# Finishing the last image of a quantised convolution block: the channel gate from sums of numerators, the last product in halves

## The chip, the cores and the metric

The kernel runs on one core of one Trainium2 chip, as one launch. The metric is the device time of one execution in microseconds. The text names the engines as the profile does: PE is TensorE, ACT is ScalarE, DVE is VectorE, POOL is GpSimd, SP is SyncE, which issues most DMAs.

## The reference

The input is `x` of shape (16, 256, 28, 28). It is normalised in 32 groups of channels, and the layer is added to `x`. Twice, a 3x3 convolution is replaced by a soft look-up: for each channel the nine values of a patch are compared with 16 centroids, a softmax over the 16 gives weights, and the weighted centroids go through a matrix.

```python
def amm_conv3x3(x, centroids, w_sub, stride=1):
    ...
    d = sum(p * p) - 2.0 * einsum('bncs,cks->bnck', p, centroids) + sum(centroids * centroids)
    attn = softmax(-d, axis=-1)
    lut = einsum('cks,cso->cko', centroids, w_sub)
    out = einsum('bnck,cko->bno', attn, lut)

def se_layer(x, w1, b1, w2, b2):
    s = mean(x, axis=(2, 3))
    s = relu(s @ w1 + b1)
    s = sigmoid(s @ w2 + b2)
    return x * s[:, :, None, None]

# y is x normalised by groups
out = relu(bn1(amm_conv3x3(y, centroids1, wsub1)))
out = bn2(amm_conv3x3(out, centroids2, wsub2))
out = relu(se_layer(out, se_w1, se_b1, se_w2, se_b2) + y)
return x + out
```

What matters here is the end of an image in the second layer: the gate `s` needs the mean of every output channel over the whole image, so it can start only when the whole image is summed up, or when those sums are got in another way. They can be: the mean over positions of a product of weights and numerators is the product of the weights and the summed numerators.

## The kernel before, in words

The 16 images are done one after the other, first all of layer one, then all of layer two. An image is four blocks: two halves of the rows (14 rows, `N` = 392 positions) times two halves of the input channels. For each block TensorE makes the logits (`lg`), ScalarE the exponentials (`e`), TensorE the sums of the denominators (`nb`) and of the numerators (`na`), VectorE the reciprocals (`r`, spread by `rb`), and VectorE, ScalarE and GpSimd the scaled numerators: nine tiles of 128 x 392, held in pairs (`qp`) and one single (`qo`).

The numerators of the four blocks then go through the weight matrices. Instead of eight block products (two row halves, two input halves, two output halves) the kernel does seven and some sums and differences, in the manner of Strassen and Winograd: `PRODUCTS` lists them (A11, S1, S3, S2, S4, A12, A22), each 9 matmuls of 128 x 392 in f32, which the profile counts as 18. GpSimd makes the differences of numerators (`mix`). The results are added up in the four regions of an image: `c11` and `c12` are the two row halves of the first 128 channels, `c21` and `c22` those of the other 128. The last two products are A12, which completes `c11`, and A22, which completes `c21`.

The schedule is written out by hand: `at(cluster, sub, function, ...)` files a step under a place in time, and the steps are issued in the order of the places. Each engine works through its own queue in that order. `g` is the first cluster of an image (8 an image), so a step of image `b` at `g + 12` stands in the middle of the next image's work, or, for the last image, at the end of all. PSUM is a ring of four tiles of two banks each (`p_ring`, tags `ps0` to `ps3`); `banks` picks the tag from `ROLES` and the step, or from `tag`, and a new tile waits until the old one of its tag has been read.

At the end of an image of layer two, `norm_out` or `norm_both` applies the batch norm on ScalarE and sums up the positions at the same time, `se_hidden` and `se_gate` make the gate (two small products on TensorE, activations on ScalarE), `se_recip` finishes the sigmoid on VectorE, `finish_norm` makes the group-normalised input again, and gate, sum, relu and final sum follow. For all images but the last this is spread over the products of the next one: `finish_gate` and `finish_relu` on ScalarE, `finish_sum` and `finish_add` on GpSimd. For the last image nothing is left to hide it, and `finish_fast` does it on VectorE in two passes for each half of the channels.

`gn_var` makes the group norm's scale: a small product, two short steps on VectorE, then the power -1/2 and a product on GpSimd. `flags` checks on VectorE that sums and centroids lie in the range for which the fast path holds; `flag_sum` adds the flags up. Every engine loads the result and branches past a fallback, which redoes everything in a safer form and does not run here.

Of the kernel before, what the change touches and what calls it, by code (L numbers as in the profile page):

```python
# [17 lines left out]
P = 128  # L18
H = W = 28
HW = H * W  # L20
# [3 lines left out]
N = RT * W  # L24
PTW = RT * PW
K = 16
S = 9
NS = 9
NST = 18
GN_EPS = 1e-5  # L30
# [8 lines left out]
KO = (2, 3, 4, 5, 6, 7, 8, 0, 1)  # L39
# [45 lines left out]
def kernel(  # L85
# [20 lines left out]
    nc = tc.nc  # L106
    B, C, _ = x.shape
    NB = C // P
# [28 lines left out]
    def bank(name, step=None, role=None, tag=None):  # L137
        return banks(name, step, role, tag)[:, 0, :]
# [28 lines left out]

    xs = {}

    def load_x(b, spare=False):  # L170
        if spare:
            t = epool.tile([P, 4, N], F32, tag="e", name="e").rearrange("p i n -> p (i n)")
            t = t.rearrange("p (b n) -> p b n", b=NB)
# [101 lines left out]
    def rsqrt(dst, src, eps, n):  # L275
        t = small.tile([P, n], F32, name="rs_t")
        nc.gpsimd.tensor_scalar(t, src, eps, None, op0=ALU.add)
        nc.gpsimd.tensor_tensor(dst, t, mhalf[:, :n], ALU.pow)
# [4 lines left out]
    bn = []  # L283
# [12 lines left out]

    cst = const.tile([P, 64], F32, name="cst")

    def small_bank(name, step):
        return bank(name, step, step and ROLES["small"][step % 2], EARLY["small"].get(step))  # L300

    def center_sq(wf, c0, w, eng=None):
        sq = rpool.tile([P, N], F32, tag="r", name="sq")
# [56 lines left out]
    def gn_var(b, k0=0, n=NB, step=None):  # L360
        gm, dv = gst.pop((b, "m"))
        ps = small_bank("gnp", step)[:, :n]
        nc.tensor.matmul(ps, lhsT=gmat, rhs=dv[:, :n], start=True, stop=True)  # L363
        var = small.tile([P, NB], F32, name="gn_var")
        neg = small.tile([P, NB], F32, name="gn_neg")
        nc.vector.tensor_scalar_mul(neg[:, :n], gm[:, :n, 0], -1.0)
        nc.vector.scalar_tensor_tensor(var[:, :n], ps, GN_EPS, gm[:, :n, 1], op0=ALU.add, op1=ALU.add)
        rstd, shift = (nrm[:, b, i, k0 : k0 + n] for i in (1, 2))
        nc.gpsimd.tensor_tensor(rstd, var[:, :n], mhalf[:, :n], ALU.pow)
        nc.gpsimd.tensor_tensor(shift, neg[:, :n], rstd, ALU.mult)  # L370

    def grid(t):
        return t.rearrange("p (r w) -> p r w", w=PW)
# [149 lines left out]
    def pair(u, mm):  # L523
        return qs["pair"][u["qi", mm]]
# [15 lines left out]

    accs = {}

    def product(key, us, w, ks, first=True, last=True, step=None):
        if first:
            accs[key] = bank("acc", step, step and ROLES["acc"][step % 2], EARLY["acc"].get(step))
        for n, k in enumerate(ks):
            nc.tensor.matmul(  # L547
                accs[key][:, :N], lhsT=wl[w][:, k, :], rhs=us["q", k],
                start=first and n == 0, stop=last and n == len(ks) - 1,
            )  # L550

# [278 lines left out]

    se = {}

    def se_hidden(b, step=None):
        ysum = ys[b, "sum"]
        ps = small_bank("sep", step)[: 2 * RED, :1]
        terms = [(k, i) for k in range(NB) for i in range(2 if b >= B - 1 else 1)]
        for k, i in terms:
            nc.tensor.matmul(  # L838
                ps, lhsT=w1_sb[:, k, :], rhs=ysum[:, k, i : i + 1],
                start=(k, i) == terms[0], stop=(k, i) == terms[-1],  # L840
            )
# [3 lines left out]
        nc.scalar.activation(se[b], halves, AF.Copy, scale=hid)  # L845

    def se_gate(b, step=None):
        ps = small_bank("sep", step)[:, :NB]
        nc.tensor.matmul(ps, lhsT=w2_sb, rhs=se[b], start=True, stop=True)  # L849
        gt = small.tile([P, NB], F32, name="se_gt")  # L850
        for k in range(NB):
            nc.scalar.activation(
                gt[:, k : k + 1], ps[:, k : k + 1], AF.Exp, bias=nb2_sb[:, k : k + 1], scale=-1.0
            )
        nc.scalar.activation(gt, gt, AF.Identity, bias=one, scale=1.0)
        se[b] = gt
# [8 lines left out]
    def finish_norm(b, k):  # L865
        if k == 0:
            if b == B - 1:
                ys[b, "t"] = epool.tile([P, 4, N], F32, tag="e", name="xn").rearrange("p i n -> p (i n)")
            else:
                ys[b, "t"] = io.tile([P, 1568], F32, tag="pb", name="xn")  # L870
        nc.scalar.activation(
            ys[b, "t"][:, HW * k : HW * k + HW], xs[b][:, k], AF.Identity,
            bias=nrm[:, b, 2, k : k + 1], scale=nrm[:, b, 1, k : k + 1],
        )
# [12 lines left out]
    def finish_fast(b, k):  # L887
# [4 lines left out]
            ys.pop((b, "t"))  # L892
        nc.vector.scalar_tensor_tensor(y, y, 0.0, xs[b][:, k], op0=ALU.max, op1=ALU.add)

    def store(b, k, dst=None, eng=None):
# [20 lines left out]
        nc.vector.memset(fl[:, 3:4], 1.0)  # L916

    def flag_sum():
        ps = bank("flp")[:, :1]
# [5 lines left out]
    def at(cl, sub, f, *a, **kw):  # L925
        jobs.setdefault((cl, sub), []).append((f, a, kw))
# [24 lines left out]
    for j, u in enumerate(blocks):  # L951
# [41 lines left out]
        for mm in (4, *kept):  # L993
            at(g, 1.2, spread, u, mm)
            at(*((g, 1.3) if j != 1 else (5, 0.06)), scale_q, u, mm)

    for l in range(2):
        for b in range(B):
            n = l * B + b
# [2 lines left out]
            for c, w, r, ks in PRODUCTS:  # L1002
                if g + c == 5:
                    for sub, k0, k1 in ((0.8, 0, 5), (0.82, 5, 7), (0.84, 7, 9)):
                        at(4, sub, product, (n, c), us[r], w, ks[k0:k1], k0 == 0, k1 == 9, step=4)
                else:
                    at(g + c, 1.32 if g + c == 7 else 2.0, product, (n, c), us[r], w, ks, step=g + c)
            for mm in (1, 2, 3, 4, 0):
                at(g + 5, 2.5 if n else {4: 0.07, 0: 0.09}.get(mm, 0.05), mix, us[0], mm, us[1], us[0])
                at(g + 7, 1.35 if mm in (4, 0) else 1.25, mix, us[1], mm, us[2], us[1])  # L1010
                at(g + 8, 1.37 if mm == 1 else 1.4, mix, us[0], mm, us[2], us[0])
                at(g + 10, 1.4, mix, us[0], mm, us[0], us[3])
# [10 lines left out]
            at(g + 12, 0.0, acc_add, l, b, c11, (n, 11))  # L1023
            at(g + 12, 2.02, acc_add, l, b, c21, (n, 12), op=ALU.subtract)
            if l == 0 or b == B - 1:
                at(g + 11, 1.9, norm_out, l, b, *c12)
                at(g + 11, 1.91, norm_out, l, b, *c22)
                at(g + 12, 1.9 if l else 0.05, norm_out, l, b, *c11)
                at(g + 13, 1.06, norm_out, l, b, *c21)
            else:  # L1030
                for o in range(NB):
                    at(g + 12 + o, 1.9, norm_both, b, o)
# [17 lines left out]
                        at(*((g + 4, 1.92) if b else (4 + 3 * q, 1.6 + 0.05 * q)), to_home1, b + 1, q)  # L1050
            else:
                last = b == B - 1
                at(*((g + 11, 0.6) if last else (g + 13, 2.6)), load_x, b, last)
                at(g + 14 - last, 2.1, se_hidden, b, g + 14 - last)
                at(*((g + 14, 1.05, se_gate, b, g + 14) if last else (g + 17, 2.1, se_gate, b, g + 17)))
                at(*((g + 14, 1.05) if last else (g + 18, 0.3)), se_recip, b)
                for q in range(NB):
                    at(*((g + 12, 0.4) if last else (g + 19, 1.9)), finish_norm, b, q)
                    if not last:
# [5 lines left out]
                    else:  # L1065
                        at(g + 14, 1.92, finish_fast, b, q)
                        at(g + 14, 1.92, store, b, q)
                if b == B - 1:
                    at(g + 11, 1.9, flags)
                    at(g + 12, 2.9, flag_sum)  # L1070

    at(0, 1.55, load_w, 0, "A11")
# [247 lines left out]
```

## Time and profile before

| | us |
|---|---|
| median of 3 runs | 2622.66 (2621.62 to 2627.43) |
| profiled execution | 2625.73 |
| its span | 2624.2 |
| mean granted TensorE clock | 0.998 of full speed |

The profile gives each engine's busy time, the chain of work that ended last, groups of instructions with their mean duration and the idle time before them (with what ended it), and a timeline by engine. A group's row reads: line, engine, operation, out <- in, shapes, xcount, then busy us and mean ns of one, then the idle time before it and its releasers. A row of the timeline reads: start, duration, engine, line, operation, and in brackets the idle time just before. `L547` is line 547 of the kernel before. A row with q behind the engine's name is the work of its sequencer. Rows of stretches give the length, then the busy time of PE, PEld, DVE, ACT and POOL with counts, then the granted clock, the DMA share and GB/s.

### The profile page before, as it was taken

What the parts mean: (1) busy time and instruction counts of PE and PEld (TensorE: products, weight loads), DVE (VectorE), ACT (ScalarE), POOL (GpSimd) and SP (SyncE); (2) the same over time, 40 slices, a digit from 0 to 9 for tenths busy, and PEclk for the clock granted to TensorE, in tenths of its full rate; (3) what the DMA queues carried; (4) which work ended last, traced back from release to release, by engine and by line L of the source; (5) the groups of instructions that cost most, each with busy time, mean ns of one, the idle gap of its engine ahead of it and who ended that gap; (6) DMA issues with size and microseconds to landing.
All of it is one profiled execution on the core that took longest, in us unless ns stands there. A gap on an engine that the chain in (4) does not pass through costs nothing.

```text
span 2624.2 us, 85651 instructions
## 1 busy us (share of the span) xinstructions
PE 2588.2 (99%) x36984; PEld 1264.5 (48%) x36984; DVE 1762.8 (67%) x3774; ACT 1360.3 (52%) x1879; POOL 1893.1 (72%) x1286
## 2 busy tenths in 40 slices
PE   6999999999999999999999999999999999999997
PEld 2444454444544444544444444444444444444444
DVE  5776656666566665566676767766776667767665
ACT  5444544444444454444455655555655556555553
POOL 3786666766568766676666887878878777878786
PEclk9999999999999999999999999999999999999999
DMA  8656656666555565554664344444344443444441
GB/s 218 159 164 177 197 149 184 171 174 173 149 144 147 170 183 177 171 156 139 179 170 105 104 116 126 118 120 119 104 120 129 123 118 106 117 122 122 116 120 47
DMA packets 217960, 374.38 MB, mean 143 GB/s; under 512 B 29752, under 2 KB 188520, under 8 KB 217576
## 3 DMA queue, kind: packets, MB, share of 16 engines
q1 hardware_dynamic: 211256, 335.24, 47.8%
q0 software_dynamic: 6320, 33.58, 3.5%
q8 instruction: 295, 4.83, 0.8%
q14 instruction: 89, 0.73, 0.1%
HBM read 288.93 MB, written 79.80 MB: 141 GB/s over the span
## 4 chain that ended last, share of the span: by engine, by line
PE 97%; DVE 1%; ACT 0%; DMA 0%; POOL 0%; issue 0%; SPq 0%; DVEq 0%; POOLq 0%; ACTq 0%
PE acc L547 52%; PE lg L412 17%; PE nb L477 14%; PE na L463 14%; DMA pt<-home 0%; DVE r L505 0%; PE sep L849 0%; ACT e L423 0%; DVE gn_st L340 0%; POOL qp L556 0%; PE sep L838 0%; DMA xt<-in_x 0%; PE gnp L346 0%; PE gnp L363 0%; DVE rb L520 0%
## 5 line engine op out<-in xcount | busy, mean ns | idle before, releaser
L547 PE MATMUL acc<-qp,wall 128*128 128x392 f32 x3072 | 1096.9, 500 | 1.0 <-DVE qp L539 0.7
L423 ACT ACTIVATE e<-lg 128x784 f32<-128x784 f32 x960 | 737.8, 821 | 637.2 <-PE lg L412 634.3
L556 POOL TENSOR_TENSOR qp<-qp,qp 128x784 f32<-128x784 f32 x512 | 943.4, 1866 | 156.1 <-DVE qp L539 155.7
L547 PEld LDWEIGHTS acc<-qp,wall 128*128 128x128 f32 x3072 | 565.2, 190 | 508.6 <-issue 60.0
L520 DVE STREAM_SHUFFLE rb<-r 128x392 f32<-128x392 f32 x1024 | 551.2, 605 | 0.0
L412 PE MATMUL lg<-pt,wd 32*32 32x392 f32 x16256 | 484.2, 502 | 6.8 <-DMA pt<-home 4.4
L491 DVE SCALAR_TENSOR_TENSOR r<-nb,kst,r 128x392 f32<-128x392 f32 x128 | 80.0, 625 | 461.1 <-ACT r L487 445.7
L477 PE MATMUL nb<-e,cwb 64*32 64x392 f32 x8192 | 376.6, 492 | 0.1
L463 PE MATMUL na<-e,cwa 64*32 64x392 f32 x8192 | 374.3, 492 | 0.0
L539 DVE TENSOR_TENSOR qp<-na,rb 128x784 f32<-128x784 f32 x352 | 333.8, 972 | 60.0 <-PE na L463 48.5
L528 POOL TENSOR_TENSOR qo<-qo,rb 128x392 f32<-128x392 f32 x128 | 132.3, 1033 | 326.8 <-DVE rb L516 326.3
L505 DVE RECIPROCAL r<-r 128x392 f32<-128x392 f32 x128 | 333.2, 2603 | 4.4
L528 POOL TENSOR_TENSOR qp<-qp,rb 128x784 f32<-128x784 f32 x160 | 295.7, 1858 | 3.6 <-issue 0.7
L477 PEld LDWEIGHTS nb<-e,cwb 64*32 64x32 f32 x8192 | 189.9, 106 | 179.0 <-issue 26.3
L463 PEld LDWEIGHTS na<-e,cwa 64*32 64x32 f32 x8192 | 182.7, 106 | 182.5 <-issue 74.5
L412 PEld LDWEIGHTS lg<-pt,wd 32*32 32x32 f32 x16256 | 121.0, 103 | 282.6 <-issue 251.0
L547 PE MATMUL acc<-qp,w_A 128*128 128x392 f32 x512 | 182.6, 499 | 0.0
L487 ACT ACTIVATE r<-nb,kst 128x392 f32<-128x392 f32 x128 | 86.7, 677 | 164.6 <-PE nb L477 164.6
L447 POOL TENSOR_TENSOR z<-z,mx 128x1568 f32<-128x1568 f32 x32 | 91.8, 2869 | 94.7 <-DVE mx L441 94.7
L547 PE MATMUL acc<-qo,wall 128*128 128x392 f32 x384 | 157.7, 492 | 0.0
L533 ACT COPY qp<-na 128x784 f32<-128x784 f32 x160 | 130.0, 813 | 26.9 <-PE na L463 25.1
L547 PEld LDWEIGHTS acc<-qp,w_A 128*128 128x128 f32 x512 | 94.5, 190 | 82.3 <-DVE qp L539 19.8
(154 smaller groups left out, 1640.1 us busy)
## 6 DMA issues: line engine op xcount, KB each, us to landing
pt<-home SPq DMA_DIRECT2D x762, 209.0 KB
pt<-home SPq DMA_DIRECT2D x762, 104.5 KB
home<-xpad SPq DMA_DIRECT2D x30, 899.0 KB
xt<-in_x SPq DMA_DIRECT2D x30, 784.0 KB
out_dram<-y SPq DMA_DIRECT2D x32, 392.0 KB
d_wS<-st SPq DMA_DIRECT2D x12, 192.0 KB
wall<-d_wS SPq DMA_DIRECT2D x4, 576.0 KB
wall<-in_ws SPq DMA_DIRECT2D x3, 576.0 KB
```

Source lines behind the costliest of these rows:

```text
L412: nc.tensor.matmul(bk[32 * c : 32 * c + 32, :N].rearrange("p (r w) -> p r w", w=W), lhsT=wts["wd", u["hh"]][32 * i : 32 * i + 32, mm, c, : ...
L423: nc.scalar.activation(eg[:, 2 * i : 2 * i + 2, :], bk[:, :, :N], AF.Exp, scale=2.0)
L447: nc.gpsimd.tensor_tensor(zk, zk, mx.unsqueeze(2).to_broadcast([P, N // 4, K]), ALU.subtract)
L463: nc.tensor.matmul(bs[32 * i : 32 * i + 32, r, :N], lhsT=wts["cwa", u["hh"]][64 * r : 64 * r + 64, mm, i, :], rhs=es[64 * r : 64 * r + 64, ...
L477: nc.tensor.matmul(bs[32 * i : 32 * i + 32, r, :N], lhsT=wts["cwb", u["hh"]][64 * r : 64 * r + 64, mm, i, :], rhs=es[64 * r : 64 * r + 64, ...
L505: nc.vector.reciprocal(u["r"], u["r"])
L520: nc.vector.stream_shuffle(rb[:, r, :], u["r"], mask_of(2 * mm + r))
L528: nc.gpsimd.tensor_tensor(q, q, u.pop(("rb", mm)), ALU.mult)
L533: nc.scalar.copy(pair(u, mm), u.pop(("na", mm))[:, :, :N])
L539: nc.vector.tensor_mul(pair(u, mm), u.pop(("na", mm))[:, :, :N], rb)
L547: nc.tensor.matmul(accs[key][:, :N], lhsT=wl[w][:, k, :], rhs=us["q", k], start=first and n == 0, stop=last and n == len(ks) - 1,)
L556: nc.gpsimd.tensor_tensor(pair(out_u, mm), pair(in0, mm), pair(in1, mm), ALU.subtract)
```

## The change

It touches the last two images of layer two, and one short step of layer one.

- **Gate of the last image.** The sums of `c11` and `c21` over their positions are no longer taken from the finished regions. `norm_ahead` norms what the two regions hold so far and sums that up. `total_act` (ScalarE) and `total_dve` (VectorE) sum the numerators of the last two products over the positions, `total_sub` turns them into the sums of the last difference, `weigh` (ScalarE, nine copies of a 128 x 128 weight tile with a scale) and `weigh_sum` (VectorE) make weighted weights of them, and `rest_sum` brings them into the right place by two small products and one VectorE step. These two products stand inside A12, after five of its nine matmuls; `se_hidden` stands after seven, `se_gate` behind A12.
- **The last product** A22 is made in two halves of 196 positions, in the two banks of one PSUM tile (`open_last`). Everything else of the last image is finished before: `norm_join`, `finish_part` and `finish_ahead`; then `finish_last` and a store for each half.
- **The preceding image** is gated into PSUM (`gate_wide`, ScalarE) and finished there by two VectorE steps (`finish_wide`) for each half of the channels, in place of two ScalarE and two GpSimd steps. Its `finish_norm` stands earlier.
- **Places**: the last image's `x` and its normalised copy go into a patch tile (`spare_of`) in place of two exponential tiles. `flags` stands later; `flag_sum` stands at the very end as before, but the last VectorE steps are now ahead of it.
- **Root**: `gn_var` keeps its shorter form only for single columns (the first image); for all others it does one step on VectorE and four on GpSimd (`rsqrt` with its own sum, product, sign) in place of two and two.

```diff
+        if n == 1:
...
+        else:
+            nc.vector.tensor_add(var[:, :n], gm[:, :n, 1], ps)
+            rsqrt(rstd, var[:, :n], GN_EPS, n)
+            nc.gpsimd.tensor_tensor(shift, gm[:, :n, 0], rstd, ALU.mult)
+            nc.gpsimd.tensor_scalar(shift, shift, -1.0, None, op0=ALU.mult)
...
+    def gate_wide(b, k):
+        ys[b, "g"] = banks("gp", tag=3)[:, :, :N]
+        y = ys[b, k].rearrange("p (t n) -> p t n", t=2)
+        nc.scalar.activation(ys[b, "g"], y, AF.Copy, scale=se[b][:, k : k + 1])
+
+    def finish_wide(b, k):
...
+        nc.vector.tensor_tensor(ps, ps, g, ALU.add)
+        nc.vector.scalar_tensor_tensor(
+            y, ps, 0.0, xs[b][:, k].rearrange("p (t n) -> p t n", t=2), op0=ALU.max, op1=ALU.add
+        )
...
+    def total_dve(u, mm):
...
+            nc.vector.tensor_reduce(qsum[:, 0, 2 * mm : 2 * mm + 2], pair(u, mm), axis=AX.X, op=ALU.add)
+
+    def total_act(u, k):
+        nc.scalar.activation(
+            spare_of(NB * S * P, N, 1), u["q", k], AF.Identity, bias=zero, scale=one, accum_out=qsum[:, 1, k : k + 1]
+        )
+
+    def total_sub():
+        nc.gpsimd.tensor_tensor(qsum[:, 1], qsum[:, 1], qsum[:, 0], ALU.subtract)
+
+    def weigh(o, ks):
+        for k in ks:
+            nc.scalar.activation(
+                spare_of((o * S + k) * P, P, 1), wl["A22" if o else "A12"][:, k, :], AF.Copy, scale=qsum[:, o, k : k + 1]
+            )
+
+    def weigh_sum(o):
+        v = spare_of(o * S * P, S * P, 1).rearrange("p (k n) -> p n k", k=S)
+        nc.vector.tensor_reduce(vsum[:, o, :], v, axis=AX.X, op=ALU.add)
+
+    def rest_sum(b, tag):
+        ps = bank("pv", tag=tag)[:, :NB]
+        for o in range(NB):
+            nc.tensor.matmul(ps[:, o : o + 1], lhsT=vsum[:, o, :], rhs=one, start=True, stop=True)
+        ys[b, "rest"] = rest[:, 1]
+        nc.vector.tensor_tensor(rest[:, 1], ps, rest[:, 0], ALU.mult)
...
+    def finish_part(b, k, n0, n1):
...
+        nc.vector.scalar_tensor_tensor(y, y, se[b][:, k : k + 1], t, op0=ALU.mult, op1=ALU.add)
+        nc.vector.scalar_tensor_tensor(y, y, 0.0, x0, op0=ALU.max, op1=ALU.add)
+
+    def finish_ahead(b):
...
+    def finish_last(b, key, n0, n1):
+        y, x0 = ys[b, 1][:, n0:n1], xs[b][:, 1, n0:n1]
+        t = ys[b, "t"][:, HW + n0 : HW + n1]
+        nc.vector.scalar_tensor_tensor(
+            y, accs.pop(key)[:, : n1 - n0], rest[:, 2, 1:2], t, op0=ALU.mult, op1=ALU.add
+        )
+        nc.vector.scalar_tensor_tensor(y, y, 0.0, x0, op0=ALU.max, op1=ALU.add)
...
+    def open_last(n):
+        bs = banks("acc", tag=2)
+        accs[n, 12], accs[n, 13] = bs[:, 0, :], bs[:, 1, :]
...
+                for k in KO:
+                    at(g + 9, 1.5, total_act, us[0], k)
+                for mm in (1, 2, 3, 4):
+                    at(g + 9, 1.5, total_dve, us[3], mm)
+                at(g + 10, 0.5, weigh, 0, KO)
+                at(g + 10, 0.52, weigh_sum, 0)
+                at(g + 10, 1.405, total_sub)
+                at(g + 10, 1.5, norm_ahead, b, 1)
+                at(g + 10, 1.51, weigh, 1, KO)
+                at(g + 11, 1.8, weigh_sum, 1)
+                at(g + 11, 1.96, rest_sum, b, 1)
+                at(g + 11, 1.98, se_hidden, b, None, 1)
+                at(g + 11, 1.995, se_gate, b, None, 1)
+                at(g + 12, 0.0, norm_join, b, (n, 11))
+                at(g + 12, 0.01, se_recip, b)
+                at(g + 12, 0.02, finish_part, b, 0, 0, HW)
+                at(g + 12, 0.03, finish_part, b, 1, N, HW)
+                at(g + 12, 0.04, finish_ahead, b)
+                for h in range(2):
+                    at(g + 12, 2.01 + 0.02 * h, finish_last, b, (n, 12 + h), N // 2 * h, N // 2 * h + N // 2)
```

More of the change, by code (lines that the diff above doesn't have):

```diff
@@ L297, with small_bank @@
     cst = const.tile([P, 64], F32, name="cst")
[L299 to L300 removed]
+    def small_bank(name, step, tag=None):
+        return bank(name, step, step and ROLES["small"][step % 2], EARLY["small"].get(step) if tag is None else tag)
     def center_sq(wf, c0, w, eng=None):
@@ L541, with product @@
     accs = {}
-    def product(key, us, w, ks, first=True, last=True, step=None):
-        if first:
-            accs[key] = bank("acc", step, step and ROLES["acc"][step % 2], EARLY["acc"].get(step))
+    def product(key, us, w, ks, first=True, last=True, step=None, cols=(0, N), tag=None):
+        if first and key not in accs:
+            accs[key] = bank("acc", step, step and ROLES["acc"][step % 2], EARLY["acc"].get(step) if tag is None else tag)
         for n, k in enumerate(ks):
             nc.tensor.matmul(
-                accs[key][:, :N], lhsT=wl[w][:, k, :], rhs=us["q", k],
+                accs[key][:, : cols[1] - cols[0]], lhsT=wl[w][:, k, :], rhs=us["q", k][:, cols[0] : cols[1]],
                 start=first and n == 0, stop=last and n == len(ks) - 1,
@@ L831, with se_hidden @@
     se = {}
-    def se_hidden(b, step=None):
+    def se_hidden(b, step=None, tag=None):
         ysum = ys[b, "sum"]
[L835 to L841, printed above, removed]
+        ps = small_bank("sep", step, tag)[: 2 * RED, :1]
+        terms = [(k, ysum[:, k, i : i + 1]) for k in range(NB) for i in range(2 if b >= B - 1 else 1)]
+        if (b, "rest") in ys:
+            terms += [(k, ys[b, "rest"][:, k : k + 1]) for k in range(NB)]
+        for n, (k, term) in enumerate(terms):
+            nc.tensor.matmul(ps, lhsT=w1_sb[:, k, :], rhs=term, start=n == 0, stop=n == len(terms) - 1)
         hid = small.tile([2 * RED, 1], F32, name="se_hid")
@@ new lines, in weigh_sum, with sum_of @@
+    def weigh_sum(o):
[3 more added lines that the diff above has]
+        ps = bank("pv", tag=tag)[:, :NB]
+        for o in range(NB):
+            nc.tensor.matmul(ps[:, o : o + 1], lhsT=vsum[:, o, :], rhs=one, start=True, stop=True)
+        ys[b, "rest"] = rest[:, 1]
+        nc.vector.tensor_tensor(rest[:, 1], ps, rest[:, 0], ALU.mult)
+    def sum_of(b, o, t):
+        if (b, "sum") not in ys:
+            ys[b, "sum"] = small.tile([P, NB, 2], F32, name="ysum")
+        return ys[b, "sum"][:, o, t : t + 1]
```

111 lines of the change are left out of this document (85 added, 26 removed).

## The prediction

> **What bounds the kernel now.** I read the page's busy shares first, then the chain of waits over the end, then the timeline of the last 60 us by engine.
>
> ```profile
> span 2624.2 us, 85651 instructions
> ...
> PE 2588.2 (99%) x36984; PEld 1264.5 (48%) x36984; DVE 1762.8 (67%) x3774; ACT 1360.3 (52%) x1879; POOL 1893.1 (72%) x1286
> ```
>
> TensorE is busy for 99% of the span, so only two kinds of edit can shorten this kernel: fewer products, or less time in which TensorE has nothing left. The change removes no product. The chain of waits shows where TensorE stands idle: at the end.
>
> ```profile
> 2582.27 2.95 PE na L463 x64
> ...
> 2585.80 6.16 PE acc L547 x18
> 2591.96 0.31 PE sep L849 x2
> 2592.27 17.99 PE acc L547 x54
> ...
> 2610.35 0.57 DVE y L586
> ...
> 2614.15 1.05 DVE y L890
> ...
> 2617.17 0.97 DVE y L893
> ```
>
> The last three products (54 passes, 0.333 us each) end at 2610.25. Then the gate runs as one chain through three engines, and VectorE finishes the image at 2618.14. These 7.9 us are all that the change can take. What follows is fixed by SyncE:
>
> ```profile
> L1166 PEldq COMPARE_BRANCH  x1: 3855/3855/3855, 2613.3 to 2613.3; - x1
> ...
> L1166 SPq COMPARE_BRANCH  x1: 50/50/50, 2619.2 to 2619.2; - x1
> ...
> L1166 SPq EVENT_SEMAPHORE  x8: 17/17/17, 2622.0 to 2622.6; - x8
> ```
>
> It issues the store, branches at 2619.2 and waits on until 2622.0; the span ends at 2624.2, that is 6.06 us after VectorE's end. A smaller last store therefore gains nothing by itself: the branch hides it. So I forecast T, the end of VectorE's last step, and add 6.06 us.
>
> **The early edits.** The longer root runs for images 1 to 15 of the first layer.
>
> ```profile
> L277 POOL TENSOR_SCALAR rs_t<-vecs 128x2 f32<-128x2 f32 x2 | 0.4, 223 | 0.1
> ...
> L370 POOL TENSOR_TENSOR nrm<-gn_neg,nrm 128x2 f32<-128x2 f32 x15 | 3.1, 204 | 1.2
> ```
>
> ```profile
> 206.66 1.10 POOL L619 DMA_INDIRECT home<-hpad,col  x1 [0.44 <-ACT hpad L598]
> ```
>
> It adds one instruction like L277 and one like L370 to GpSimd's queue, 0.43 us an image, and takes one small one from VectorE. Queued behind it is the scatter of the other half image, which in the sampled image has 0.44 us to spare because it waits for ScalarE; ScalarE normalises the next image only about a stage later. Cost taken: 0. If that cover were gone: 15 x 0.43 = 6.5 us at most.
>
> **The tail, on the clock of this profile.** TensorE's order up to the last three products stays. The first of four products (S2, 2585.80) now takes the PSUM tag that VectorE's first evacuation frees, not its second:
>
> ```profile
> 2583.81 2.72 DVE L539 TENSOR_TENSOR qp<-na,rb 128x784 f32<-128x784 f32 x3
> ...
> 2583.98 0.82 ACT L533 COPY qp<-na 128x784 f32<-128x784 f32 x1 [6.14 <-PE na L463]
> ...
> 2585.80 4.19 PE L547 MATMUL acc<-qp,wall 128*128 128x392 f32 x12 [0.66 <-DVE qp L539]
> ...
> 2592.00 1.04 DVE L584 TENSOR_TENSOR y<-acc,y 128x392 f32<-128x392 f32 x2 [3.94 <-PE acc L547]
> ...
> 2592.31 0.41 ACT L852 ACTIVATE se_gt<-sep,nb_sb 128x1 f32<-128x1 f32 x2 [7.51 <-PE sep L849]
> ...
> 2593.28 1.79 ACT L863 ACTIVATE y<-y,se_gt 128x784 f32<-128x784 f32 x2 [0.23 <-DVE se_gt L859]
> 2594.97 1.96 ACT L871 ACTIVATE xn<-xt,nrm 128x784 f32<-128x784 f32 x2
> ...
> 2598.97 1.28 DVE L908 TENSOR_SCALAR ok<-wsum 128x128 f32<-128x128 f32 x1
> 2599.09 0.71 ACT L602 ACTIVATE y<-y,bnsh,bnsc 128x392 f32<-128x392 f32 x1 [2.16 <-DVE y L584]
> ...
> 2601.10 1.85 POOL L556 TENSOR_TENSOR qp<-qp,qp 128x784 f32<-128x784 f32 x1
> ...
> 2604.72 0.06 DVE L916 MEMSET fl<- 128x1 f32 x1
> ```
>
> The first of three evacuations ends near 2584.75, before the numerators end (2585.22), so of the 0.66 us wait 0.55 goes: S2 starts at 2585.25, S4 at 2591.72, A12 at 2597.72.
>
> ScalarE's new early work (four norms at 0.98, two sign copies at about 0.2, one L602-like at 0.71: 5.0 us) fits into its 6.14 us of idle time ahead of 2583.98. The nine total_act then take 9 x 0.71 = 6.4 us, until 2591.2, within the 7.51 us of idle time. The last image's x now goes to a patch tile whose last reader on TensorE is done before the last block's numerators start, so the load is early enough. For the reductions and the small copies these groups give the prices:
>
> ```profile
> L441 DVE TENSOR_REDUCE mx<-z 128x98 f32<-128x1568 f32 x32 | 56.9, 1777 | 0.0
> ...
> L863 ACT ACTIVATE y<-y,se_gt 128x784 f32<-128x784 f32 x30 | 26.9, 952 | 0.2 <-DVE se_gt L859 0.2
> ...
> L502 DVE SCALAR_TENSOR_TENSOR qo<-nb,kst,qo 128x392 f32<-128x392 f32 x128 | 67.7, 529 | 0.0
> ...
> L845 ACT ACTIVATE se_hh<-halves,se_hid 32x2 f32<-32x2 f32 x16 | 4.7, 294 | 0.5
> ...
> L893 DVE SCALAR_TENSOR_TENSOR y<-y,e 128x784 f32<-128x784 f32 x2 | 1.9, 974 | 0.1
> ...
> L912 DVE TENSOR_SCALAR csum<-csum 128x2 f32<-128x2 f32 x1 | 1.2, 1192 | 0.0
> ...
> L646 DVE TENSOR_REDUCE pk<-c 128x16 f32<-128x144 f32 x2 | 0.8, 404 | 0.1
> ...
> L910 DVE TENSOR_REDUCE fl<-ok 128x1 f32<-128x256 f32 x1 | 0.4, 420 | 0.0
> ...
> L911 DVE TENSOR_SCALAR fl<-fl 128x1 f32<-128x1 f32 x1 | 0.2, 153 | 0.0
> ```
>
> A reduction costs 0.155 us + 1.03 ns an element (L441 against L910): 0.97 for 784, 0.56 for 392. total_dve's first four (3.5 us) fit into VectorE's 3.94 us of idle time; the fifth delays the reciprocal of image 14's gate by 0.95, and ScalarE's gate_wide starts at 2593.65.
>
> A weigh copy of 128 elements lies between L845 (0.29) and L863 (0.95 for 784): 0.40 by itself. Two L863 start 0.845 apart, 0.11 less than one lasts, so in a row 0.30 each; bounds 0.25 and 0.40. Then ScalarE: gate_wide to 2594.5, weigh(0) 9 x 0.30 to 2597.2, norm_ahead to 2597.9, weigh(1) to 2600.6, its last result at 2600.7.
>
> weigh_sum reduces 1152 elements: 1.35 us; by the strided L646, which has 0.25 us for 144 elements beyond the 0.155, it would be 2.15. Most of VectorE's reads here are of whole rows, so I take 1.35. weigh_sum(1) ends at 2602.1.
>
> **First new wait.** TensorE reaches the two pv products after 10 passes of A12, at 2601.05, and stands until 2602.15: 1.1 us. What is behind them in its queue, the rest of A12, the gate and A22, waits too. Then pv 0.3, 4 passes 1.33, six se_hidden products of two passes 0.66 (by 0.22 for four), 4 passes 1.33, gate 0.31: the gate's product ends at 2606.1, and ScalarE has its sum at 2606.95. The first half of A22 takes 18 passes of half the width, 18 x 0.167 = 3.0, and ends at 2609.1.
>
> ```profile
> 2566.36 0.22 PE sep L838 x4
> ```
>
> ```profile
> L547 PEld LDWEIGHTS acc<-qp,wall 128*128 128x128 f32 x3072 | 565.2, 190 | 508.6 <-issue 60.0 <-POOL qp L556 22.1 <-DVE qp L539 19.8
> ```
>
> A weight load shows 190 ns, longer than a half pass; were it the limit, a half would take 18 x 0.19 = 3.4. I take 3.0 and keep 3.4 for the range. [...]
>
> **VectorE becomes the chain.** From ScalarE's weigh(1): two norms 1.4 and gate_wide 0.9, to 2602.9; then VectorE, with no gap: finish_wide 2.0 (to 2604.95); the flags; norm_join 0.57; reciprocal 0.17; finish_part of 784 1.05 + 0.97; of 392 2 x 0.53; finish_ahead 0.1 + 0.53; the first read of A22's first half 0.31 (by L502 and L893, 1.1 ns an element). The flags take 5.8 us before (2598.97 to 2604.78), because steps such as L912 (1.19 us for two elements) end just when a GpSimd step ends; before, GpSimd's last mix is over at 2602.95 and image 14's sums follow it. Those sums leave GpSimd, so nothing of it runs beside the flags at 2604.95, and I price them at L910's 0.42 and eight at 0.15: 1.65. With gaps of 0.02 to 0.05, that first read ends at 2604.95 + 1.65 + 0.57 + 0.17 + 2.05 + 1.08 + 0.65 + 0.33 = 2611.45.
>
> **Second new wait.** The two halves of A22 lie in two banks of one tile, and in the changed program the second half's first pass waits for VectorE's first read of the first half. So TensorE stands from 2609.1 to 2611.5, 2.4 us, does the second half until 2614.5, and VectorE adds 0.1 + 0.33 + 0.36: T = 2615.3.
>
> Sum: 2618.14 - 2615.3 = 2.8 us gained. The flag now comes last, so all five engines load it and branch together; TensorE's branch (3.86 us) would start about T + 0.8 and end at T + 4.7, where SyncE's last of these waits stood at 2622.6, T + 4.5. I give 0.2 us back. Against the profiled execution (2625.73 us, span 2624.2) that makes 2623.1 us; against the median of 2622.66, 3.1 us lower, it makes **2620.0 us**.
>
> **Rivals.** (1) *VectorE is in time.* If the weigh copies run at 0.25, the first wait vanishes; if besides VectorE reaches its first read by 2609.1, the second half follows at once, T = 2609.1 + 3.0 + 0.8 = 2612.9, gain 5.2 less the 0.2: 2617.6. For: ScalarE's overlap is read from long steps. Against: VectorE has 8.5 us to do after 2602.9, with no gap to give.
>
> (2) *The new work is longer.* weigh at 0.40 moves everything by 1.8 us, a strided weigh_sum by 0.8: T = 2617.9, no change: 2622.6.
>
> (3) *TensorE's clock halves in the new waits.*
>
> ```profile
> 2614.25:2614.50 0.25, 0.00 (x0) 0.00 (x0) 0.25 (x1) 0.00 (x0) 0.00 (x0) 0.50 0.30 66
> ```
>
> ```profile
> 29.95 3.30 PE L412 MATMUL lg<-pt,wd 32*32 32x392 f32 x64 [4.42 <-DMA pt<-home]
> ```
>
> The granted clock (the third number from the end of the stretch) is at 0.50 by 2614.25, 4.0 us after the last long pass, though a few short products ran in between; and after 4.42 us of idle time at the start 64 passes took 3.30 us. If waits of 1.1 and 2.4 us with busy time around them suffice, the second half takes 6.0 instead of 3.0, and if it halves at the first as well, another 1.7: T = 2620.0, 2624.7, slower than before. It decides from the point where idle time of about 2.4 us counts as idle. [...]
>
> (4) *The early root is not hidden*: plus up to 6.5 us, 2626.5.
>
> **How the numbers follow.** Forecast 0.56; rival 1 0.15; rival 2 0.17; rival 3 0.08; rival 4 0.04. About 0.2%, 5.2 us, is what a measurement of this kernel can tell from no change (its three runs lie 5.8 us apart). Faster by more needs all of rival 1: half of it and some spread, 0.12. Slower by more needs rival 3 or 4 at their worst: 0.06. Within: 0.82. The range leaves out the worst ends: 2616.6 (rival 1 and 1 us of spread) to 2624.6 (rival 3).
>
> **What would show it.** In the profile of the changed kernel: S2 without its 0.66 us wait; TensorE idle ahead of pv by about 1 us, released by VectorE's weigh_sum; idle again ahead of A22's second half by about 2.4 us, released by the read of the first; flags under 2 us; no branch later than SyncE's. Wrong, if the second half follows the first at once, if TensorE waits anywhere before the last image, or if the clock column drops ahead of the last pass.

## The result and the profile after

The changed kernel takes 2628.07 us (median; 2623.49 to 2630.84) against 2623.55 us (2621.46 to 2627.43) for the kernel before: 1.0015 times its time, 95% interval 1.0009 to 1.0021, that is 2.4 to 5.5 us slower. The forecast was 2620.0 us, 2.7 us below the 2622.66 us known then. The profiled execution took 2629.22 us, its span 2627.7 us at a mean granted clock of 0.996.

Where the last image begins in the span differs by up to 6 us between the traces below (2577.1 to 2583.0 us); the kernel before and e2, the same program up to there, are 5 us apart. So two traces are compared from one event that lies ahead of the change: the start of the last block's numerators on TensorE. On the timelines of the kernel before and of the changed one it stands at:

```profile
2582.20 2.94 PE L463 MATMUL na<-e,cwa 64*32 64x392 f32 x64
```

```profile
2582.98 2.94 PE L471 MATMUL na<-e,cwa 64*32 64x392 f32 x64
```

The changed kernel's chain of waits from there (start, length, what), its line numbers some eight higher at the products:

```profile
2585.91 6.14 PE acc L555 x18
...
2601.03 2.18 DVE pt L948
...
2603.26 0.38 PE pv L953 x2
...
2607.05 0.32 PE sep L856 x2
...
2612.26 0.43 DVE y L992
...
2612.74 3.27 PE acc L555 x18
...
2616.48 0.36 DVE y L995
2616.84 0.06 DVE fi L1026
```

Up to VectorE's last step on the image this is what the change promised: it ends at 2616.84, 33.86 us behind the numerators' start, against 35.94 before (2618.14 - 2582.20). 2.08 us are gained. But the chain's last row is new: the cast of the flag `fi`. And the span ends 10.86 us behind the image's last step, where it was 6.06 us.

Those 10.86 us are in the rows of the sequencers at the end of the program (duration min/median/max in ns, then the first and the last start). First the kernel before:

```profile
L1164 POOLq TENSOR_LOAD <-fi x1: 922/922/922, 2611.0 to 2611.0; - x1
...
L1316 POOLq DRAIN  x3: 46/103/6607, 2614.7 to 2624.0; - x3
L1316 SPq DRAIN  x3: 7/7/13, 2623.4 to 2623.7; - x3
```

and the changed one:

```profile
L1318 POOLq TENSOR_LOAD <-fi x1: 502/502/502, 2616.9 to 2616.9; - x1
...
L1320 POOLq INC_SWDGE_SEM  x1: 1796/1796/1796, 2618.4 to 2618.4; - x1
...
L1470 POOLq EVENT_SEMAPHORE  x4: 17/17/17, 2626.9 to 2627.6; - x4
L1470 POOLq DRAIN  x3: 46/103/6607, 2620.2 to 2627.4; - x3
L1470 SPq DRAIN  x3: 7/7/13, 2622.5 to 2627.1; - x3
```

GpSimd's way out is long: it loads `fi` (0.5 us), branches, spends 1.8 us in INC_SWDGE_SEM and then drains for 6.607 us. Before, `fi` was cast ahead of the last gate, so GpSimd set out at 2611.0 and was through its long drain at 2621.3 (2614.7 + 6.6), 2.1 us ahead of SyncE's first drain at 2623.4. Now every engine gets `fi` behind the last image step: SyncE is at its drain at 2622.5, GpSimd is in its long drain until 2626.8 (2620.2 + 6.6), and the closing semaphores follow from 2626.9 on. 2.1 us gained and 4.8 lost make 2.7 us between these two executions, inside the measured 2.4 to 5.5 but near its lower end.

### The profile page after: what moved, and what is told of

The parts are those of the page before. It is cut to its first block, busy times and chain, and to the rows that moved or that the text cites. A ratio compares the mean times of both kernels' runs of the same rounds, so it can differ in the third digit from the quotient of the medians.

```text
span 2627.7 us, 85784 instructions
## 1 busy us (share of the span) xinstructions
PE 2588.0 (98%) x37010; PEld 1267.1 (48%) x37010; DVE 1770.5 (67%) x3776; ACT 1371.4 (52%) x1915; POOL 1893.6 (72%) x1313
## 4 chain that ended last, share of the span: by engine, by line
PE 96%; DVE 1%; DMA 1%; POOL 1%; ACT 1%; SPq 0%; issue 0%; POOLq 0%; DVEq 0%; ACTq 0%
PE acc L555 51%; PE lg L420 17%; PE nb L485 14%; PE na L471 14%; DMA pt<-home 0%; POOL qp L564 0%; SPq L406 0%; ACT pt L942 0%; DVE r L513 0%; PE sep L856 0%; ACT e L431 0%; PE sep L848 0%; DMA home<-xpad 0%; DMA xt<-in_x 0%; DVE rb L528 0%
## 5 line engine op out<-in xcount | busy, mean ns | idle before, releaser
L555 PE MATMUL acc<-qp,wall 128*128 128x392 f32 (+1 forms) x3088 | 1099.4, 499 | 4.4 <-DVE y L992 2.2
L555 PE MATMUL acc<-qo,wall 128*128 128x392 f32 (+1 forms) x386 | 157.9, 491 | 0.0
```

The source lines that it names most:

```text
L555: nc.tensor.matmul(accs[key][:, : cols[1] - cols[0]], lhsT=wl[w][:, k, :], rhs=us["q", k][:, cols[0] : cols[1]], start=first and n == 0, s ...
```

## The experiments

**Theory A**: GpSimd's way out starts when `fi` is cast and takes a fixed time, so that the end is the later of two: the last image step + 5.9 us (SyncE), or the cast of `fi` + 10.8 us (GpSimd). Against it stand B (the joint branch of all engines is slow by itself), C (the longer root of the early images is what costs) and D (the end hangs on the branches of other engines or on GpSimd, and not on VectorE's last step). The short names e1 to e12 are those of the table. All distances below are from the start of the last numerators, from the timelines, in us; ratios are to the kernel before on the same chip.

| kernel | numerators start | last image step ends | span ends | time against before, 95% |
|---|---|---|---|---|
| before | 2582.20 | 35.94 | 42.0 | 1 |
| changed | 2582.98 | 33.86 | 44.7 | 1.0015 (1.0009 to 1.0021) |
| e1_flag_early | 2579.98 | 33.87 | 39.7 | 0.9994 (0.9984 to 1.0003) |
| e2_before_flag_last | 2577.14 | 35.95 | 46.8 | 1.0019 (1.0010 to 1.0028) |
| e5_short_root | 2579.99 | 33.87 | 44.7 | 1.0008 (0.9999 to 1.0017) |
| e6_flag_mid | 2578.20 | 33.86 | 40.9 | 0.9997 (0.9988 to 1.0006) |
| e3_two_banks | 2580.20 | 31.62 | 37.5 | 0.9986 (0.9977 to 0.9995) |
| e8_whole_product | 2577.92 | 31.98 | 38.0 | 0.9991 (0.9982 to 1.0000) |
| e4_pv_later | 2579.31 | 30.69 | 36.6 | 0.9980 (0.9970 to 0.9990) |
| e9_rows_sum | 2579.42 | 33.18 | 39.1 | one run, 2619.93 us |
| e4b_flags_beside_pool | 2579.73 | 41.29 | 47.4 | 1.0008 (0.9999 to 1.0017) |
| e12_image14_gpsimd | 2578.77 | 39.48 | 46.7 | 1.0012 (1.0003 to 1.0021) |

**The flag early (e1).**

```diff
-                    at(g + 12, 2.9, flag_sum)
+                    at(g + 12, 0.005, flag_sum)
```

> The changed kernel with flag_sum (one product of one column and the cast to fi) issued right behind norm_join instead of last; nothing else moves. Theory A (GpSimd's way out, from the load of fi to the end of its 6.6 us drain, some 10 us long, ends the changed kernel because fi is cast last): GpSimd is through at about 2618, SyncE's way out ends the kernel again, 5.7 to 6.1 us behind VectorE's last step; that step itself stands within 0.2 us of where it was; 4.2 to 4.8 us faster than the changed kernel, so about 2623.5 us, 0 to 2 us above or below the kernel before. Rival B (all five engines branch out of the body together and hold each other up, so that the end is late whatever GpSimd does): VectorE's end to the end of the span stays above 9 us and the time within 1 us of the changed kernel's. Rival C (the longer root of the early images is what costs): no change to the changed kernel.

Measured 2621.85 us, 6.2 us below the changed kernel's median (5.5 by the two ratios) and 2.0 below the kernel before in its own runs (2623.87; the interval does not exclude zero). The last image step stands where it was (33.87). Its exit rows:

```profile
L1318 POOLq TENSOR_LOAD <-fi x1: 493/493/493, 2605.0 to 2605.0; - x1
...
L1470 POOLq DRAIN  x3: 46/103/6607, 2608.2 to 2619.5; - x3
L1470 SPq DRAIN  x3: 7/7/13, 2618.8 to 2619.2; - x3
```

GpSimd's drain of the same 6.607 us is over at 2614.8, and SyncE's at 2618.8 is the last one again, as in the kernel before. The tail is 5.0 us shorter by this one move, a little more than the 4.2 to 4.8 us expected, and only 5.9 us lie behind the last image step. B, which kept that distance above 9 us, falls, and so does C as the cause of the loss.

**The flag last in the kernel before (e2).** The same move the other way.

```diff
-                    at(g + 12, 2.9, flag_sum)
+                    at(g + 14, 2.5, flag_sum)
```

> The kernel before with flag_sum alone moved from ahead of the last gate to behind the last image's steps, as the last work of the program. Theory A: VectorE's last step of the image stays at its place, but GpSimd now loads fi about 0.4 us behind it and needs some 10 us more: the distance from VectorE's last step to the end of the span grows from 6.06 to about 10.9 us, the kernel gets 4.5 to 5 us slower than before. Rival B (joint branch, but only together with the new tail): 0.2 us slower at most, as the prediction gave for it. Rival C: no change.

Measured 2628.94 us against 2623.87: 5.1 us slower. VectorE's last image step is where it was (35.95), and 10.81 us lie behind it:

```profile
L1164 POOLq TENSOR_LOAD <-fi x1: 496/496/496, 2613.2 to 2613.2; - x1
...
L1316 POOLq DRAIN  x3: 46/103/6607, 2616.5 to 2623.6; - x3
L1316 SPq DRAIN  x3: 7/7/13, 2619.2 to 2623.3; - x3
```

So the place of the flag costs the kernel before, without any of the new steps, what it costs the changed one.

**The flag between the halves (e6).**

```diff
-                    at(g + 12, 2.9, flag_sum)
+                    at(g + 12, 2.015, flag_sum)
```

> The changed kernel with flag_sum between the two halves of the last product: fi is cast about 3.7 us ahead of VectorE's last step. Theory A gives the end as the later of two: VectorE's last step + 5.7 to 6.1 us, or fi's cast + 10.8 us. Here the second is about 0.9 us later than the first: 0.5 to 1.5 us slower than with the flag early, 3 to 4 us faster than the changed kernel. Rival B: as the flag early, or as the changed kernel, not between them with this amount.

```profile
2608.22 0.14 DVE L1026 CAST fi<-flp 1x1 int32<-1x1 f32 x1
```

```profile
L1470 POOLq DRAIN  x3: 46/103/6607, 2611.7 to 2618.8; - x3
L1470 SPq DRAIN  x3: 7/7/13, 2617.1 to 2618.6; - x3
```

GpSimd's long drain (2611.7 + 6.6) now ends 1.2 us behind SyncE's first. The cast ends at 2608.36 and the span at 2619.1, 10.7 us later; from the last image step it is 7.0. The tail is 1.2 us longer than with the flag early and 3.8 shorter than in the changed kernel, the median of 2622.92 us is 1.1 above e1's. From the cast's end to the span's end it is 10.8 in the changed kernel, 10.75 in e2 and 10.7 here: one price in three places. B gives no such end in between.

**The short root (e5).** `gn_var` as in the kernel before for all images:

```diff
-        if n == 1:
+        if True:
```

> The changed kernel with the short root of the kernel before for all images of the first layer. Theory A and the prediction: within 1 us of the changed kernel, since the two GpSimd steps are hidden; the end of the last numerators in the span moves by less than 0.5 us. Rival C: 3 to 6.5 us faster than the changed kernel, all of it ahead of the last image.

Measured 2626.49 us; the tail is the changed kernel's to 0.1 us. The intervals of the two ratios, 1.0008 and 1.0015, overlap, but by themselves would leave room for several us. The traces are narrower. From the first block's numerators to those of the 65th, which is all of layer one, the three traces with the short root take 1278.0 to 1282.2 us on TensorE's timeline (this one 1278.7) and the nine with the longer one 1278.8 to 1282.4 (e1 1279.1); the shortest of each kind are 0.8 us apart. The 3 to 6.5 us of rival C are not there; a cost of one us or so would not be seen.

**The second wait taken away (e3).** The second half goes to A12's old bank.

```diff
-        accs[n, 12], accs[n, 13] = bs[:, 0, :], bs[:, 1, :]
+        accs[n, 12], accs[n, 13] = bs[:, 0, :], banks("acc", tag=0)[:, 0, :]
```

> As the kernel with the early flag (e1), but the second half of the last product goes to a bank of another tile (the one that A12 has left), so that its first pass no longer waits for VectorE's read of the first half. Theory A (behind VectorE's last step come 5.8 us of SyncE's way out, so what moves that step moves the end one for one): the wait of 2.0 us ahead of the second half is gone; VectorE's last step ends 31.7 us behind the start of the last numerators instead of 33.87; 2.1 us faster than e1, about 2619.7 us. Rival D (the end hangs on the other engines' branches, 3.5 us for TensorE's, or on GpSimd, not on VectorE's last step): less than 0.5 us faster than e1 though the wait is gone.

**The last product whole (e8).**

```diff
-                        at(g + c, 2.0 + 0.02 * h, product, (n, 12 + h), us[r], w, ks, cols=(N // 2 * h, N // 2 * h + N // 2))
+                    at(g + c, 2.0, product, (n, 12), us[r], w, ks, tag=2)
...
+                at(g + 12, 2.01, finish_last, b, (n, 12), 0, N)
+                at(g + 12, 2.01, store_part, b, 1, 0, N)
```

> As e1, but the last product A22 whole: 18 passes of full width into one bank, one read, one store for the two halves. The prediction's step that halves are half as long: a half measured 3.27 us instead of 3.0, so two cost 6.5 against 6.0 whole. Theory A: without the wait between halves VectorE's last step comes 31.7 us behind the start of the last numerators (24.4 + 6.0 + 1.25), as with two banks: 2.1 us faster than e1, within 0.3 us of e3. Rival (the halves are what hides VectorE's work, as the change's words have it): as e1 or slower.

Both take the wait away, and the last image step comes 2.25 and 1.9 us earlier (31.62, 31.98); the span's end follows by 2.2 and 1.7 us. The medians are 2620.47 and 2621.50 us; by the ratios that is 2.1 and 0.8 us below e1, and each ratio's own interval is 2.4 us to either side, so the traces tell here and the times only do not contradict. Rival D falls with them. First the halves of e3, then the whole product of e8:

```profile
2604.73 2.26 PE L555 MATMUL acc<-qp,wall 128*128 128x196 f32 x12
...
2610.14 0.83 PE L555 MATMUL acc<-qp,wall 128*128 128x196 f32 x4
```

```profile
2602.43 4.22 PE L555 MATMUL acc<-qp,wall 128*128 128x392 f32 x12
...
2607.15 1.48 PE L555 MATMUL acc<-qp,wall 128*128 128x392 f32 x4
```

Two halves one behind the other take 6.2 us (2604.73 to 2610.97), as long as one whole product (2602.43 to 2608.63). So a half that is followed at once takes half as long: the same pass of the two halves starts 2.99 us apart (2606.82 and 2609.81 in e3). The 3.27 us that one shows by itself are 0.28 more, the end of its last pass, which otherwise overlaps the next product. The split is thus worth 0.4 us (31.62 against 31.98), by its shorter last reads (0.42 and 0.36 us in e3, 0.63 and 0.57 in e8). With the wait between the halves, as in e1, it costs 1.9 us.

**The first wait filled (e4).**

```diff
-                    for sub, k0, k1 in ((1.95, 0, 5), (1.97, 5, 7), (1.99, 7, 9)):
+                    for sub, k0, k1 in ((1.95, 0, 7), (1.97, 7, 9)):
...
-                    at(g + c, 2.0, product, (n, 12), us[r], w, ks, tag=2)
+                    at(g + 11, 1.99, product, (n, 12), us[r], w, ks[:2], True, False, tag=2)
+                    at(g + c, 2.0, product, (n, 12), us[r], w, ks[2:], False, True)
```

> As e8, with TensorE's order around the gate changed: the pv products (which wait 1.38 us for VectorE) four passes later, the last four passes of A12 between them and the gate's first products, four passes of A22 between those and the gate's last two. Theory A: the 1.38 us wait is filled with passes that come later otherwise; TensorE waits 0 to 0.4 us for the flag instead; VectorE's chain (ready 29.3 us behind the start of the last numerators) becomes the limit, its last step ends at 30.4: 1.2 us faster than e8, 5.4 us below the kernel before, about 2618.3 us. Rival: the gate gets later by what is put ahead of it (1.3 us), VectorE's last step at 31.7, as e8.

TensorE's timeline has no idle time left, and VectorE, ready at 2608.52, waits 0.24 us for it:

```profile
2599.25 0.75 PE L953 MATMUL pv<-one,pt 128*128 128x1 f32 x4
2599.86 1.56 PE L555 MATMUL acc<-qp,wall 128*128 128x392 f32 x4
...
2608.76 0.63 DVE L992 SCALAR_TENSOR_TENSOR y<-acc,rest,pt 128x392 f32<-128x392 f32 x1 [0.24 <-PE acc L555]
```

The gate comes no later, the last image step 1.3 us earlier than in e8 and 0.3 us later than expected, because TensorE and not VectorE sets it. Measured 2617.95 us, 0.9980 (0.9970 to 0.9990): this version is faster than the kernel before by 5.3 us. TensorE is its bound again up to the last product.

**weigh_sum over rows (e9).** Same copies, written interleaved.

```diff
-                spare_of((o * S + k) * P, P, 1), wl["A22" if o else "A12"][:, k, :], AF.Copy, scale=qsum[:, o, k : k + 1]
+                spare_of(o * S * P, S * P, 1).rearrange("p (n k) -> p n k", k=S)[:, :, k], wl["A22" if o else "A12"][:, k, :], AF.Copy, scale=qsum[:, o, k : k + 1]
```

> As e1, but weigh writes its nine copies interleaved (element n of copy k at 9 n + k), so that weigh_sum reduces whole rows instead of a strided view. The prediction's two prices: 1.35 us if the stride is what costs, 2.2 us as measured if it is not. In the first case the wait ahead of pv falls from 1.38 to about 0.5 us and VectorE's last step comes 0.8 us earlier; the copies then write with a stride, 0.30 us each if that costs ScalarE nothing.

The timeline of the changed kernel, then of this one:

```profile
2601.03 2.17 DVE L948 TENSOR_REDUCE pt<-pt 128x128 f32<-128x1152 f32 x1 [0.67 <-ACT pt L942]
...
2603.26 0.38 PE L953 MATMUL pv<-one,pt 128*128 128x1 f32 x2 [1.38 <-DVE pt L948]
```

```profile
2597.61 1.35 DVE L948 TENSOR_REDUCE pt<-pt 128x128 f32<-128x1152 f32 x1 [1.50 <-ACT pt L942]
...
2599.01 0.38 PE L953 MATMUL pv<-one,pt 128*128 128x1 f32 x2 [0.69 <-DVE pt L948]
```

The same reduction takes 1.35 us over whole rows, 2.17 over a view with 512 bytes between elements: it is the stride. The wait ahead of pv halves and the last image step comes 0.7 us earlier (33.18); nine copies into a stride of 36 bytes take 2.85 us instead of 2.73.

**The flags beside GpSimd's work (e4b).**

```diff
-                    at(g + 11, 2.2, flags)
+                    at(g + 10, 0.51, flags)
```

> As e4, with the nine flag steps moved on VectorE from behind image 14's last step (where GpSimd is idle) to ahead of the first weigh_sum (where GpSimd is at its last mixes). The prediction's reason for pricing the flags at 1.65 us and not at the 5.8 us that they took before: beside GpSimd's steps VectorE's small ones are held up. If that is so, the flags take 4 to 6 us here, both weigh_sums come 3 to 5 us later, TensorE waits ahead of pv again, and VectorE's last step comes 2 to 4 us later than in e4. If GpSimd has no part in it, the flags take 1.65 us here too, weigh_sum 0 starts about 1 us late, VectorE gains 1.65 us later on, and its last step comes 0 to 0.4 us earlier than in e4.

```profile
2593.71 1.74 DVE L1013 TENSOR_SCALAR ok<-wsum 128x128 f32<-128x128 f32 x1
2595.38 1.88 DVE L1014 TENSOR_SCALAR ok<-wsum 128x128 f32<-128x128 f32 x1
2597.29 0.42 DVE L1015 TENSOR_REDUCE fl<-ok 128x1 f32<-128x256 f32 x1
...
2598.59 1.38 DVE L1020 TENSOR_TENSOR fl<-fl 128x1 f32<-128x1 f32 x1
```

GpSimd's mixes beside them:

```profile
2593.51 3.67 POOL L564 TENSOR_TENSOR qp<-qp,qp 128x784 f32<-128x784 f32 x2
...
2598.10 1.85 POOL L564 TENSOR_TENSOR qp<-qp,qp 128x784 f32<-128x784 f32 x1
```

The nine steps take 6.27 us (2593.71 to 2599.98) instead of 1.65, and three long ones end just as one of GpSimd's mixes ends (2595.4, 2597.2, 2599.95). Some steps are held up and others are not: the two tensor-scalar steps of 128 elements (1.74 and 1.88 us, 0.22 each in the changed kernel) and the tensor-tensor step (1.38 against 0.16) are, the reduction (0.42 us in both places) and two tensor-scalar steps of one element (0.15 in both) are not. What sets the two kinds apart is not shown. The last image step, though, came 10.6 us later than in e4 and not 2 to 4. TensorE is through with the pv products 4.7 us later (25.4 us behind the start of the last numerators against 20.7); the rest is its clock, on its timeline and in its stretches (the third number from the end is the granted clock):

```profile
2604.97 2.96 PE L555 MATMUL acc<-qp,wall 128*128 128x392 f32 x4
```

```profile
2604.00:2604.50 0.50, 0.00 (x0) 0.00 (x0) 0.47 (x1) 0.50 (x1) 0.00 (x0) 0.53 0.00 0
...
2617.50:2618.00 0.50, 0.50 (x3) 0.33 (x2) 0.00 (x0) 0.00 (x0) 0.00 (x0) 0.81 0.54 190
```

TensorE stood idle for 2.67 and 1.65 us with two short products between; the clock fell 4.2 us behind the last long pass, four passes then took 2.96 us instead of 1.56, and it was back only at 2617.7, 13 us after TensorE had work again. This is rival 3 of the prediction, in another kernel. By the times this version is only 2.1 us slower than the kernel before (interval -0.3 to 4.5), by its one trace 5.4; whether the clock falls in every execution is not shown.

**Image 14 by the old way (e12).**

```diff
-                near = b == B - 2
+                near = False
```

(The tag of its gate stays.)

> As e1, with image 14 finished as in the kernel before (gate and norm on ScalarE, two sums each on GpSimd) and not through PSUM on VectorE; its two norms stand late on ScalarE again. VectorE loses two steps pairs (3.9 us), but GpSimd works until about 30 us behind the start of the last numerators, so the flags run beside it, and ScalarE's sums for the gate come about 1.5 us later. Theory A: end of the span = the later of VectorE's last step + 5.85 us and GpSimd's last step + 10.8 us, that is 40.5 to 42 us behind the start of the last numerators against 39.7 for e1: 1 to 2.5 us slower than e1. Rival: image 14 is off the critical path and only VectorE's share counts: as e1, or faster by up to 1 us.

The tail is 7.0 us longer than e1's, not 1 to 2.5:

```profile
2605.00 2.50 DVE L982 SCALAR_TENSOR_TENSOR y<-y,pt 128x784 f32<-128x784 f32 x1
2607.43 2.19 DVE L981 SCALAR_TENSOR_TENSOR y<-y,se_gt,pt 128x392 f32<-128x392 f32 x1
```

```profile
2611.41 4.29 PE L555 MATMUL acc<-qp,wall 128*128 128x196 f32 x12 [4.75 <-DVE y L992]
```

```profile
2610.25:2610.50 0.25, 0.00 (x0) 0.00 (x0) 0.25 (x2) 0.00 (x0) 0.00 (x0) 0.50 0.00 0
```

Beside GpSimd's two last sums, VectorE's steps take 2.50 and 2.19 us where they take 0.97 and 0.62. (The flags, too, take 4.8 us instead of 1.65, but VectorE saves the 3.9 us of image 14.) Its first read is 2.9 us later, TensorE's wait grows to 4.75 us, its clock halves 3.5 us behind the last pass, and the second half takes 6.0 us instead of 3.3. That makes the 5.6 us by which the last image step is late. Another 1.4 us lie behind that step: SyncE loads `fi` 1.4 us behind it instead of 0.4. Its queue shows why:

```profile
2618.70 0.88 SPq L1001 DMA_DIRECT2D out_dram<-y  x2
```

```profile
L1318 SPq TENSOR_LOAD <-fi x1: 780/780/780, 2619.6 to 2619.6; - x1
```

The two stores of image 14 stand behind the last image's in the schedule, and SyncE issues both before it loads the flag. GpSimd's way out, which I had named as the end here, was not it. Neither was ScalarE late: TensorE waited 0.41 us for its sums. With image 14 back on GpSimd the tail is 4.7 us longer than in the kernel before (46.7 against 42.0), so the rest of the change does not pay without that part.

## Why the prediction was wrong

*What bounds the kernel, and how much can be had*: right. TensorE is busy for 98 to 99% in every version, layer two up to the last numerators takes 1260.8 or 1260.9 us in all twelve traces, and what the edits moved is in the tail.

*Early root at nothing*: nothing against it down to about one us (e5).

*S2 without its wait*: right; its row follows the numerators with no idle time. *ScalarE's early work*: the nine sums start 0.87 us apart and not 0.71, since each is followed by a read of its accumulator of 0.19 us; that group's row alone did not show it. Nothing hung on it: ScalarE's second weigh ended within 0.4 us of the forecast.

*weigh_sum*: mis-sized. I had both prices, 1.35 from whole rows and 2.15 from the strided L646, and took the first because most of VectorE's reads here are of whole rows, though this view is strided. It measured 2.18, and e9 shows that the stride is why. *The first wait* was 1.38 us instead of 1.1.

*The flags at 1.65 us* and their reason: right, in place (2605.66 to 2607.32) and by e4b.

*VectorE as the chain, and the second wait*: right in kind. On the clock of the profile before, the first read ended at 2611.90 instead of 2611.45, mostly for 0.31 us in which VectorE waited for the gate; the wait was 2.20 instead of 2.4. The passes of a half follow each other as fast as priced (e3: 18 in 2.99 us, 0.166 each), so the weight load's 3.4 us, kept for the range, was not the limit; the 3.0 us left out 0.27 us, the end of the last pass, which counts where nothing follows at once. T came to 2616.06 instead of 2615.3: 2.1 us gained of the 2.8.

*The end behind T*: **this step failed**. "I give 0.2 us back" was 4.8. "What follows is fixed by SyncE" was read from a profile in which GpSimd had set out early, and it holds only then. I saw that the flag would come last and that all engines would load it together, but I followed only the branches of TensorE and SyncE. On that path the forecast was near: SyncE's first drain came 5.7 us behind the last image step against 5.2 before. The row that decides stood in the profile before: GpSimd's drain of 6.607 us, started by the same flag 7 us ahead of the last image step, and hidden by that. e1, e2 and e6 show its price from both kernels and in between.

*The rivals*: 1 did not come, since VectorE was late; of 2 the strided reduction came, the slow copies did not; 4 is not seen. 3 did not happen here: the clock stood at 1.00 through the wait of 2.20 us, which ended at 2612.74:

```profile
2612.50:2613.00 0.50, 0.26 (x1) 0.27 (x2) 0.47 (x2) 0.00 (x0) 0.00 (x0) 1.00 0.95 354
```

That was a near thing. Behind the last product, with nothing to follow, the clock fell after 2.4 us in e6, 2.8 in the changed kernel and up to 4.6 in e3. The rows of e6, TensorE's last passes (they end at 2611.21) and the stretch of the fall:

```profile
2610.39 0.83 PE L555 MATMUL acc<-qp,wall 128*128 128x196 f32 x4
```

```profile
2613.50:2614.00 0.50, 0.00 (x0) 0.00 (x0) 0.00 (x0) 0.00 (x0) 0.00 (x0) 0.62 0.17 49
```

A mean of 0.62 between 1.00 and 0.50 puts the fall at 2613.62. The clock stood through waits of 1.99 (e1), 2.08 (e6) and 2.20 us, the last only 0.2 us short of the earliest fall, so that rival 3 stayed away may be luck. It also stood through the 2.67 us of e4b's first wait, so no single length of idle time after which it falls is shown. The 0.08 for this rival was my estimate: in the trace then known the clock was at 0.50 by 4.0 us after the last long pass and passes were slow behind 4.42 us of idle time; it showed nothing on shorter waits. None of the four rivals held the mechanism that came.

## What to carry to other kernels

At the end of a program, ask of every engine how long its own way out is and what starts it: a value that all engines load is not done when it is computed, and its place is to be priced by the longest queue behind it (10.7 to 10.8 us of GpSimd's here). Compare tails from an event ahead of the change, since the spans of single executions differ by more than the edit (the last block's numerators start anywhere from 2577.1 to 2583.0 us here). And where a wait is added on TensorE, look at its length twice: for itself, and for whether the clock survives it (it stood through 2.20 us in the changed kernel and halved in the 4.75 us of e12).

## What was not expected of the hardware

- GpSimd's long drain took 6.607 us and its INC_SWDGE_SEM 1.8 us in every trace here, whenever they began; where GpSimd was last (the changed kernel, e2, e5, e6), 10.7 to 10.8 us lay between the cast of the flag and the end of the span.
- Once the clock had halved it came back slowly: 5.6 us (e12) and 13 us (e4b) after TensorE had work again, by its records without a gap.
- A VectorE step of 0.22 us took 1.88 beside GpSimd (e4b), one of 0.97 took 2.50 (e12); `finish_wide`, with one operand in PSUM, ran its two steps at 0.98 beside GpSimd's mixes (2595.05 to 2597.04 in the changed kernel).
